# Second layer of a graph network: the split product, the rounding engine and the order of a chunk's steps

## The chip, the cores and the metric

One core of one Trainium2 chip. The metric is the device time of one execution in microseconds, as the median of the runs; lower is better. The engines are TensorE (PE; PEld is its weight load), VectorE (DVE), ScalarE (ACT), GpSimd (POOL) and SyncE (SP), which issues most DMAs. An engine's name with a q behind it is its instruction queue.

## The reference

Two graph layers with pre-norm over 12500 nodes of 128 values and 400000 edges that are sorted by destination. The first is an edge MLP with sums per destination. The second, cut to what matters here:

```python
h = jnp.maximum(_layernorm(x, axis=-1), 0.0)
H = jnp.einsum('ni,rio->rno', h, W)            # 8 relations, 128 x 128 each
msg = (H[etype, src] + b[etype]) * norm        # 400000 messages of 128
out = jax.ops.segment_sum(msg, dst, num_segments=h.shape[0])
x = x + jax.nn.relu(out)
```

`norm` is a weight per edge. All data are float32.

## The kernel before

**Work of the second layer.** The first layer's nodes go into a table in DRAM, `tab_h`, with RX = 9 blocks of 128 values in each row: eight blocks `H[r] + b[r]` for the eight relations and, as the ninth, the node's new x (`rows_h`, lines 546 to 567). Seen as rows of one block each (`tab_hr`), the message of an edge is row `src * 9 + etype`; these indices are prepared during the first layer (`hidx`, cast to integers in `hidx_sb` at line 646).

Edges are cut into tiles of P = 128, chunks of CT = 8 tiles (1024 edges) and spans of SC = 3 chunks; there are 3128 tiles, 391 chunks and 131 spans, the last of one chunk. A span's destinations lie within a window of 128 nodes. Within one partition of a chunk the eight edges stand in their order, so they have at most two destinations, the first edge's and the last's.

**One chunk** (`layer1_once`, lines 956 to 1040). GpSimd issues eight indirect DMAs, one a tile, which gather 128 rows of 512 bytes into `hg` (line 1019; five buffers). VectorE multiplies the 128x1024 tile by the edges' weights, twice: once with the weights of the edges that have the first destination (q = 0) and once with the rest (q = 1) (line 1026, into `v` in PSUM). After each product it sums the eight tiles (line 1030) into `sm`, also in PSUM. ScalarE copies `sm` to `hm` in SBUF and rounds it to fp32r, TensorE's fast float format (line 1033). VectorE subtracts to get the part lost in rounding (line 987) and builds two 128x128 one-hot matrices from the two destinations (line 989). TensorE multiplies one by the other into `acc` of the span (line 994).

These last steps are `sum_up`. The program puts them off by one chunk: a chunk's call goes into the list `todo` and runs behind the next chunk's first product.

**End of a span.** `write` reduces `acc` to the sums (line 505), takes relu and adds x, which an SP DMA has read from the table (`x1_of`, line 848), and stores the 128 rows of output (`to_out`, lines 853 and 854). Nodes that a span shares with the next are added by two small matmuls (`carry`, line 500) from the sums before.

**Order.** A scheduler orders the instructions of each engine unless the program pins them. `in_order(start, engines)` pins: it ties each instruction since `start` to the one before it on the same engine, without a wait on the chip. It looks at the list of the block that was current at the kernel's start. `layer1_once` stands in the body of an `If` on a flag (line 1044), whose instructions are collected in a block of their own, so that by the code the call at its end finds none of them.

The flag says whether the edges fit the windows above; otherwise the loops of `again` would run. They don't run here.

Of the kernel before, what the change touches and what calls it, by code (L numbers as in the profile page):

```python
# [14 lines left out]
OP = mybir.AluOpType  # L15
AX = mybir.AxisListType
ENG = mybir.EngineType
# [3 lines left out]
P = 128  # L21
D = 128
DE = 64
R = 8
# [5 lines left out]
NP = P * NJ  # L30
GJ = 7
CT = 8
CE = CT * P
SC = 3
ST = SC * CT
NT = -(-E // P)
NC = -(-E // CE)
# [12 lines left out]
ROW = 4 * D  # L50
# [3 lines left out]
def gnn_kernel(  # L54
# [34 lines left out]


    nc = tc.nc
    block = nc.cur_bb
    queues = {}

    def traced():
        return len(block.bb.instructions)

    def in_order(start, *engines):

        for i in block.bb.instructions[start:]:  # L100
            if i.engine in engines:
                if i.engine in queues:
                    tc.add_manual_dep(
                        i, queues[i.engine].name,
                        mybir.DependencyInfo(mybir.DependencyClass.NoSync,
                                             mybir.DependencyReason.DATA), reason="in order")
                queues[i.engine] = i

    start = traced()
# [8 lines left out]
    tab_h = dram.tile([NP + P, RX * D], F32, name="tab_h")  # L118
# [24 lines left out]
    b_f = const.tile([P, R * D], F32, name="b_f")  # L143
# [23 lines left out]
    def in_bytes(v):  # L167
        return v.bitcast(U8)
# [20 lines left out]
    with tc.tile_pool(name="n0", bufs=2) as pool, \  # L189
# [48 lines left out]
        for i, (xg, (g, n)) in enumerate(zip(xs, groups)):  # L238
# [4 lines left out]
            k = g - g0  # L243
# [302 lines left out]
    def rows_h(pool, psum, to, x0, aw, banks, out_row=None):  # L546

        ht = pool.tile([P, RX * D], F32, name="ht1", bufs=2)
        x1 = ht[:, R * D:]
        nc.vector.tensor_add(x1, x0, aw)  # L550
        if out_row is not None:
            nc.sync.dma_start(out[ds(out_row, P), :], x1)
        mv, sd = deviation(pool, x1)
        yield
        t = normed(pool, x1, mv, sd)
        yield
        pt = psum.tile([P, 512], F32, name=banks[0])
        nc.tensor.transpose(pt[:, 0:P], t, ident)
        hT = pool.tile([P, P], F32, name="hT1", bufs=2)
        nc.scalar.activation(hT, pt[:, 0:P], AF.Relu)  # L560
        for k in range(2):
            cols = slice(512 * k, 512 * k + 512)
            yield
            ph = psum.tile([P, 512], F32, name=banks[1 + k])
            nc.tensor.matmul(ph, hT, w_f[:, cols], start=True, stop=True)
            nc.vector.tensor_add(ht[:, cols], ph, b_f[:, cols])  # L566
        nc.sync.dma_start(to, in_bytes(ht))


    with tc.tile_pool(name="e0", bufs=2) as pool, \  # L570
# [39 lines left out]
        def prepare():  # L610

            nc.sync.dma_start(w_f.rearrange("i (r o) -> i r o", r=R), w.rearrange("r i o -> i r o"))
            yield
            nc.sync.dma_start(b_f, b.to_broadcast([P, R * D]))
            yield
            for g in range(0, NTP, QT):
                m = min(QT, NTP - g)
                cols = slice(g, g + m)
                for given, table in ((dst_t, dst_d), (et, hidx_d), (ew, ew_d)):
                    raw = pool.tile([P, QT], F32, name="raw", bufs=1)  # L620
                    nc.sync.dma_start(raw[:, :m] if given is ew else raw[:, :m].bitcast(I32),
                                      given[:, cols])
                    yield
                    if given is dst_t:
                        nc.vector.tensor_copy(raw[:, :m], raw[:, :m].bitcast(I32))
                    elif given is et:
                        nc.vector.scalar_tensor_tensor(raw[:, :m], src_sb[:, cols], float(RX),
                                                       raw[:, :m].bitcast(I32),
                                                       op0=OP.mult, op1=OP.add)
                    tr = pool.tile([P, QT], F32, name="tr", bufs=1)  # L630
                    nc.vector.transpose(tr[:, :m], raw[:, :m])
                    rows = table[cols, :].rearrange("(q r) (a j) -> a r q j", r=32, j=32)
                    for a in range(4):
                        nc.sync.dma_start(
                            rows[a], tr[32 * a:32 * a + 32, :m].rearrange("r (q j) -> r q j", j=32))
                    yield
            odd = pool.tile([P, NSP // QS], F32, name="odd", bufs=1)
            for i, s in enumerate(range(0, NSP, QS)):
                cols = slice(s * ST, (s + QS) * ST)
                hidx = pool.tile([P, QS * ST], F32, name="hidx", bufs=1)  # L640
                for table, to in ((dst_d, rel_t[:, cols]), (hidx_d, hidx), (ew_d, ew_sb[:, cols])):
                    nc.sync.dma_start(to.rearrange("p (c k) -> p c k", k=CT),
                                      table[cols, :].rearrange("(c t) (q k) -> (t q) c k",
                                                               t=CT, k=CT))
                    yield
                nc.vector.tensor_copy(hidx_sb[:, cols], hidx)
                rel = rel_t[:, cols]
                nc.vector.tensor_sub(rel.rearrange("p (s t) -> p s t", t=ST),
                                     rel.rearrange("p (s t) -> p s t", t=ST),
                                     base[:, s:s + QS, None].to_broadcast([P, QS, ST]))  # L650
                yield
                rel = rel.rearrange("p (c k) -> p c k", k=CT)
                off = []
                for k in (0, CT - 1):
                    o = pool.tile([P, QS * SC, CT], F32, name="off")
                    nc.vector.tensor_sub(o, rel,
                                         rel[:, :, k:k + 1].to_broadcast([P, QS * SC, CT]))
                    off.append(o)
                nc.vector.tensor_mul(off[0], off[0], off[1])
                nc.vector.tensor_mul(off[0], off[0], off[0])  # L660
                nc.vector.tensor_reduce(odd[:, i:i + 1], off[0].rearrange("p c k -> p (c k)"),
                                        AX.X, OP.max)
                yield
            most = pool.tile([P, 1], F32, name="most", bufs=1)
            nc.vector.tensor_reduce(most, odd, AX.X, OP.max)
            nc.sync.dma_start(odd_d.rearrange("o p -> p o"), most)
            yield
            odds = pool.tile([1, P], F32, name="odds", bufs=1)
            nc.sync.dma_start(odds, odd_d)
            yield  # L670
            nc.vector.tensor_reduce(vm[:, 1:2], odds, AX.X, OP.max)
            worst = pool.tile([1, 1], F32, name="worst", bufs=1)
            nc.vector.tensor_reduce(worst, vm, AX.X, OP.max)
            nc.vector.tensor_scalar(bad, worst, 0.0, None, op0=OP.is_gt)
            yield
            zeros = pool.tile([P, D], F32, name="zeros", bufs=1)
            nc.vector.memset(zeros, 0.0)
            nc.sync.dma_start(tab_h[NP:NP + P, R * D:], zeros)

        class Span:  # L680

# [163 lines left out]
    def x1_of(pool, rows):  # L845

        xw = pool.tile([P, D], F32, name="xw1", bufs=3)
        nc.sync.dma_start(in_bytes(xw), rows[:, R * ROW:])
        return xw

    def to_out(pool, sums, xw, to):
# [104 lines left out]
    def layer1_once():  # L956
# [4 lines left out]
        with tc.tile_pool(name="e1", bufs=2) as pool, \  # L961
# [2 lines left out]
            io_p = psum.tile([P, 512], F32, name="io_p", bufs=1)  # L964
            iota_p = io_p[:, 0:P]
            nc.vector.tensor_copy(iota_p, iota_f)
            todo = []
            open_s = []
            before = [None]

# [32 lines left out]
            for c in range(NC):  # L1003
# [19 lines left out]
                t = c % (WS * SC) * CT  # L1023
                for q in range(2):
                    v = psum.tile([P, CT, D], F32, name="v1", bufs=1)
                    nc.vector.tensor_tensor(  # L1026
                        v, hg, w_p[:, q, t:t + CT, None].to_broadcast([P, CT, D]), op=OP.mult)
                    if todo:
                        sum_up(*todo.pop())
                    nc.vector.tensor_reduce(sm[:, q, :], v.rearrange("p t d -> p d t"),  # L1030
                                            AX.X, OP.add)
                hm = pool.tile([P, 2, 2, D], F32R, name="hm2", bufs=6)
                nc.scalar.copy(hm[:, :, 0, :], sm)  # L1033
                ends = rel_t[:, c * CT:c * CT + CT:CT - 1][:, :, None]
                todo.append((s, acc, sm, hm, ends, k == 0, k == SC - 1 or c == NC - 1))
                if len(open_s) > 1 and (k == SC - 1 or c == NC - 1):
                    write()
            sum_up(*todo.pop())
            write()
            in_order(start, ENG.SP, ENG.DVE, ENG.Activation, ENG.PE)  # L1040

    flag = nc.values_load(bad[0:1, 0:1], min_val=0, max_val=1,
                          skip_runtime_bounds_check_because="it is 0 or 1")
# [66 lines left out]
```

## Time and profile before

| | us |
|---|---|
| median of 5 runs | 7953.2 (7951.66 to 7957.37) |
| the profiled execution | 7955.49 |
| its span in the trace | 7953.7 |
| first gather of the second layer starts | 4031.5 |
| last gather of the second layer starts | 7936.1 |
| mean length of a gather on GpSimd, second layer | 0.944 |
| VectorE busy between 5000 and 6000 us | 567.8 |
| GpSimd busy between 5000 and 6000 us | 755.9 |
| ScalarE busy between 5000 and 6000 us | 37.3 |

How to read it: the span is what the trace holds of one execution; the execution's own time is a little more. Busy time is the time in which an instruction ran on an engine; an engine that is busy three quarters of the time may still never wait for another, if it pauses between its own instructions. A group of instructions has its line in the code, engine, operation, what it writes and reads, and behind the bar its busy time, the mean of one in ns, and the idle time before it with what ended that. The chain that ended last is followed back from the last instruction, at each step to what released it.

### The profile page before, as it was taken

How to read it: one execution, taken by the hardware profiler on the slowest of the kernel's cores; microseconds unless marked ns; L12 is line 12 of the kernel's file. 1: busy time of each engine (PE TensorE's matmuls, PEld its weight loads, DVE VectorE, ACT ScalarE, POOL GpSimd, SP SyncE). 2: the span in 40 equal slices, each digit the busy share in tenths (PEclk: the TensorE clock that was granted, in tenths of full speed). 3: DMA queues.
4: the chain of work that ended last, by engine and by line, in shares of the span. 5: the costliest groups of instructions: out<-in, count | busy, mean ns of one | idle time of the engine just before them, and what ended most of it. 6: DMA issues, size and time to landing. Idle time of an engine off the chain costs nothing.

```text
span 7953.7 us, 56126 instructions
## 1 busy us (share of the span) xinstructions
PE 3688.1 (46%) x13981; PEld 1812.7 (23%) x13982; DVE 5276.7 (66%) x8291; ACT 1689.7 (21%) x3217; POOL 5953.6 (75%) x6273
## 2 busy tenths in 40 slices
PE   4888888888888888888820111111111101111111
PEld 2443443433444434333310000000000000000000
DVE  7887777777777777777755555555555555555555
ACT  3443333333333333333300000000000000000000
POOL 6777777777777777777757777777777777777776
PEclk7999898989999899899965555555555555555555
DMA  5555433333333333333322222222222222222222
GB/s 162 139 103 102 92 92 94 86 91 94 83 94 93 85 94 88 89 94 85 93 55 57 57 57 57 57 57 57 57 57 57 57 57 57 57 57 57 57 57 53
DMA packets 605554, 614.49 MB, mean 77 GB/s; under 512 B 361632, under 2 KB 465892, under 8 KB 604766
## 3 DMA queue, kind: packets, MB, share of 16 engines
q0 software_dynamic: 200192, 256.65, 15.1%
q1 hardware_dynamic: 403064, 353.77, 14.8%
q8 instruction: 114, 1.87, 0.1%
q14 instruction: 220, 1.80, 0.1%
q10 hardware_dynamic: 1964, 0.41, 0.0%
HBM read 509.91 MB, written 100.43 MB: 77 GB/s over the span
## 4 chain that ended last, share of the span: by engine, by line
POOL 49%; issue 23%; DVE 11%; DMA 10%; PE 5%; ACT 2%; DVEq 0%; POOLq 0%; ACTq 0%; SPq 0%
POOL hg L1019 32%; POOL gb L387 17%; DMA gb<-tab_a,src_sb 8%; DVE ohT L406 2%; DVE nm L480 2%; DVE oh L485 2%; DMA hg<-tab_h,hidx_sb 1%; DVE z L431 1%; PE pq L466 1%; PE acc L494 1%; ACT nm L475 1%; DVE pq L474 1%; DVE agT L427 1%; PE pm L442 1%; DVE ht L566 1%
## 5 line engine op out<-in xcount | busy, mean ns | idle before, releaser
L1019 POOL DMA_INDIRECT hg<-tab_h,hidx_sb x3128 | 2952.7, 944 | 996.7 <-issue 938.8
L387 POOL DMA_INDIRECT gb<-tab_a,src_sb x3032 | 2868.5, 946 | 925.6 <-issue 795.9
L1026 DVE TENSOR_TENSOR v<-hg,io_p 128x1024 f32<-128x1024 f32 x782 | 959.9, 1228 | 1621.1 <-DMA hg<-tab_h,hidx_sb 1612.2
L994 PE MATMUL acc<-hm,oh 128*128 128x256 f32 x782 | 347.5, 512 | 3516.0 <-DVE oh L989 3482.8
L994 PEld LDWEIGHTS acc<-hm,oh 128*128 128x128 f32 x782 | 205.7, 303 | 3676.8 <-issue 3641.7
L1030 DVE TENSOR_REDUCE sm<-v 128x128 f32<-128x1024 f32 x782 | 958.5, 1226 | 9.0
L1033 ACT CAST hm<-sm 128x256 fp32r<-128x256 f32 x391 | 145.7, 373 | 3777.3 <-DVE sm L1030 3777.3
L466 PE MATMUL pq<-w_n,h 128*128 128x256 f32 x3128 | 849.9, 421 | 0.0
L466 PEld LDWEIGHTS pq<-w_n,h 128*128 128x128 f32 x3128 | 649.6, 218 | 91.5 <-issue 0.9
L480 DVE SCALAR_TENSOR_TENSOR nm<-pq,nm 128x512 fp32r<-128x512 f32 x782 | 503.7, 686 | 243.8 <-ACT nm L475 214.0
L494 PE MATMUL acc<-nm,oh 128*128 128x256 f32 x3128 | 595.7, 329 | 110.8 <-DVE nm L480 66.4
L494 PEld LDWEIGHTS acc<-nm,oh 128*128 128x128 f32 x3128 | 466.3, 214 | 503.7 <-issue 207.0
L474 DVE TENSOR_TENSOR pq<-pq,b_n 128x512 f32<-128x512 f32 x782 | 509.5, 693 | 50.2 <-PE pq L466 50.0
L447 ACT ACTIVATE em<-pm,b_e 128x512 f32<-128x512 f32 x782 | 492.1, 681 | 207.4 <-PE pm L442 207.0
L459 ACT ACTIVATE h<-u,b_n 128x512 f32<-128x512 f32 x391 | 268.7, 687 | 1257.9 <-PE u L456 1257.9
L427 DVE STREAM_TRANSPOSE agT<-gb 128x256 f32<-128x256 f32 x391 | 173.5, 444 | 529.6 <-DMA gb<-tab_a,src_sb 516.0
L475 ACT ACTIVATE nm<-pq 128x512 fp32r<-128x512 f32 x782 | 432.4, 591 | 351.5 <-DVE pq L474 349.1
L420 PE MATMUL pre<-eats,w_ea 128*64 128x512 f32 x782 | 459.0, 671 | 98.6 <-DMA win<-tab_cb 93.2
L442 PE MATMUL pm<-h,w_e 32*128 32x512 f32 x1564 | 496.6, 714 | 1.0 <-ACT h L435 1.0
L406 DVE TENSOR_TENSOR ohT<-relb,io_p 126x1024 bf16<-126x1024 bf16 x391 | 477.6, 1222 | 18.4 <-DMA relb<-rel_d 6.4
L485 DVE TENSOR_TENSOR oh<-io_p,rel_s 128x1024 fp32r<-128x1024 f32 x391 | 476.0, 1217 | 0.0
L456 PE MATMUL u<-em,w_msg 128*64 128x512 f32 x1564 | 405.0, 596 | 3.3 <-ACT em L447 3.3
(122 smaller groups left out, 3474.8 us busy)
## 6 DMA issues: line engine op xcount, KB each, us to landing
eats<-in_ea SPq DMA_DIRECT2D x131, 768.0 KB
relb<-rel_d SPq DMA_DIRECT2D x131, 756.0 KB
tab_h<-ht SPq DMA_DIRECT2D x131, 576.0 KB
hg<-tab_h,hidx_sb POOLq DMA_INDIRECT x3128
gb<-tab_a,src_sb POOLq DMA_INDIRECT x3032
win<-tab_cb SPq DMA_DIRECT2D x391, 23.6 KB
xt<-in_x SPq DMA_DIRECT2D x131, 64.0 KB
xw<-tab_h SPq DMA_DIRECT2D x131, 64.0 KB
```

Of the source, the lines that this page charges most:

```text
L387: nc.gpsimd.indirect_dma_start(out=gb[:, t, :], out_offset=None, in_=tab_a, in_offset=bass.IndirectOffsetOnAxis(ap=idx(t), axis=0))
L406: nc.vector.tensor_tensor(self.ohT, relb, self.node.to_broadcast([WR, CE]), op=OP.is_equal)
L442: nc.tensor.matmul(pm, w_e2[rows, :], self.h1[rows, :], start=True, stop=True)
L466: nc.tensor.matmul(pq[:, 2 * i:2 * i + 2, :], self.h2[:, P * (2 * k + i):P * (2 * k + i) + P], w_n2, start=True, stop=True)
L474: nc.vector.tensor_add(pq, pq, b_n2[:, None, :].to_broadcast([P, 4, D]))
L480: nc.vector.scalar_tensor_tensor(nm[:, :, 1, :], pq, 0.0, nm[:, :, 0, :], op0=OP.max, op1=OP.subtract)
L485: nc.vector.tensor_tensor(self.oh, self.iota[:, None, :].to_broadcast([P, CT, P]), rel[:, :, None].to_broadcast([P, CT, P]), op=OP.is_equal)
L494: nc.tensor.matmul(acc, self.oh[:, i, :], self.nm[:, at, :, :].rearrange("p q d -> p (q d)"), start=(start and i == 0), stop=(stop and i = ...
L994: nc.tensor.matmul(acc[:, 0:2 * D], oh[:, q, :], hm[:, q, :, :].rearrange("p r d -> p (r d)"), start=begin and q == 0, stop=stop and q == 1)
L1019: nc.gpsimd.indirect_dma_start(out=hg[:, t - c * CT, :], out_offset=None, in_=tab_hr, in_offset=bass.IndirectOffsetOnAxis(ap=hidx_sb[:, t: ...
L1026: nc.vector.tensor_tensor(v, hg, w_p[:, q, t:t + CT, None].to_broadcast([P, CT, D]), op=OP.mult)
L1030: nc.vector.tensor_reduce(sm[:, q, :], v.rearrange("p t d -> p d t"), AX.X, OP.add)
```

## The change

- `in_order` takes the block that is current where the order begins, and in the second layer it pins SP, VectorE and TensorE (ScalarE has no instruction there any more).
- A chunk's first product (q = 0) is split: the last tile first, then the other seven. The second product stays whole.
- VectorE copies and rounds `sm` to `hm`, not ScalarE.
- `sum_up` runs at the end of its own chunk, not behind the next chunk's first product. `write` runs in the first chunk of the next span, ahead of that chunk's `sum_up`.
- In the table's rows, x is the first block, not the last; the indices of the messages are one more, which takes an addition where a cast was.

```diff
     nc = tc.nc
-    block = nc.cur_bb
     queues = {}
 
     def traced():
-        return len(block.bb.instructions)
+        block = nc.cur_bb
+        return block, len(block.bb.instructions)
 
     def in_order(start, *engines):
 
-        for i in block.bb.instructions[start:]:
+        block, at = start
+        for i in block.bb.instructions[at:]:
...
         ht = pool.tile([P, RX * D], F32, name="ht1", bufs=2)
-        x1 = ht[:, R * D:]
+        x1 = ht[:, 0:D]
...
-            nc.vector.tensor_add(ht[:, cols], ph, b_f[:, cols])
+            nc.vector.tensor_add(ht[:, D:][:, cols], ph, b_f[:, cols])
...
-                nc.vector.tensor_copy(hidx_sb[:, cols], hidx)
+                nc.vector.tensor_scalar(hidx_sb[:, cols], hidx, 1.0, None, op0=OP.add)
...
-            nc.sync.dma_start(tab_h[NP:NP + P, R * D:], zeros)
+            nc.sync.dma_start(tab_h[NP:NP + P, 0:D], zeros)
...
-        nc.sync.dma_start(in_bytes(xw), rows[:, R * ROW:])
+        nc.sync.dma_start(in_bytes(xw), rows[:, 0:ROW])
...
-            todo = []
             open_s = []
...
                     v = psum.tile([P, CT, D], F32, name="v1", bufs=1)
-                    nc.vector.tensor_tensor(
-                        v, hg, w_p[:, q, t:t + CT, None].to_broadcast([P, CT, D]), op=OP.mult)
-                    if todo:
-                        sum_up(*todo.pop())
+
+                    for at, n in ((CT - 1, 1), (0, CT - 1)) if q == 0 else ((0, CT),):
+                        nc.vector.tensor_tensor(
+                            v[:, at:at + n, :], hg[:, at:at + n, :],
+                            w_p[:, q, t + at:t + at + n, None].to_broadcast([P, n, D]), op=OP.mult)
                     nc.vector.tensor_reduce(sm[:, q, :], v.rearrange("p t d -> p d t"),
                                             AX.X, OP.add)
                 hm = pool.tile([P, 2, 2, D], F32R, name="hm2", bufs=6)
-                nc.scalar.copy(hm[:, :, 0, :], sm)
+                nc.vector.tensor_copy(hm[:, :, 0, :], sm)
                 ends = rel_t[:, c * CT:c * CT + CT:CT - 1][:, :, None]
-                todo.append((s, acc, sm, hm, ends, k == 0, k == SC - 1 or c == NC - 1))
-                if len(open_s) > 1 and (k == SC - 1 or c == NC - 1):
+                if k == 0 and s:
                     write()
-            sum_up(*todo.pop())
+                sum_up(s, acc, sm, hm, ends, k == 0, k == SC - 1 or c == NC - 1)
             write()
-            in_order(start, ENG.SP, ENG.DVE, ENG.Activation, ENG.PE)
+            queues.clear()
+            in_order(start, ENG.SP, ENG.DVE, ENG.PE)
```

## The prediction

> **What bounds the kernel now.** I read the page from its totals to the chain that ended last, then the second layer's groups, then the trace of one chunk and of the end. Totals and chain first:
>
> ```profile
> PE 3688.1 (46%) x13981; PEld 1812.7 (23%) x13982; DVE 5276.7 (66%) x8291; ACT 1689.7 (21%) x3217; POOL 5953.6 (75%) x6273
> ...
> POOL 49%; issue 23%; DVE 11%; DMA 10%; PE 5%; ACT 2%; DVEq 0%; POOLq 0%; ACTq 0%; SPq 0%
> ```
>
> The chain is GpSimd's busy time plus "issue", the pause between two of its instructions for which the profile shows no wait. The groups say which instructions these are (busy, mean ns of one, idle before and its releaser):
>
> ```profile
> L1019 POOL DMA_INDIRECT hg<-tab_h,hidx_sb x3128 | 2952.7, 944 | 996.7 <-issue 938.8
> ...
> L1026 DVE TENSOR_TENSOR v<-hg,io_p 128x1024 f32<-128x1024 f32 x782 | 959.9, 1228 | 1621.1 <-DMA hg<-tab_h,hidx_sb 1612.2
> ...
> L1030 DVE TENSOR_REDUCE sm<-v 128x128 f32<-128x1024 f32 x782 | 958.5, 1226 | 9.0
> L1033 ACT CAST hm<-sm 128x256 fp32r<-128x256 f32 x391 | 145.7, 373 | 3777.3 <-DVE sm L1030 3777.3
> ```
>
> GpSimd issues one gather after another and waits for nobody: of its 996.7 us of idle, 938.8 are issue pauses of 0.30 us. VectorE waits 1612.2 us for gathered rows, ScalarE 3777.3 us for VectorE. One chunk in the timeline (start us, length us; idle before and its releaser in brackets):
>
> ```profile
> 5011.73 0.94 POOL L1019 DMA_INDIRECT hg<-tab_h,hidx_sb  x1 [0.30 <-issue]
> 5011.92 1.23 DVE L1026 TENSOR_TENSOR v<-hg,io_p 128x1024 f32<-128x1024 f32 x1 [4.39 <-DMA hg<-tab_h,hidx_sb]
> 5012.98 0.94 POOL L1019 DMA_INDIRECT hg<-tab_h,hidx_sb  x1 [0.30 <-issue]
> 5013.06 0.41 DVE L987 TENSOR_TENSOR hm<-sm,hm 128x256 fp32r<-128x256 f32 x1
> 5013.40 0.41 DVE L989 TENSOR_TENSOR oh<-io_p,rel_t 128x256 fp32r<-128x256 f32 x1
> ...
> 5016.24 1.23 DVE L1030 TENSOR_REDUCE sm<-v 128x128 f32<-128x1024 f32 x1
> ...
> 5017.59 0.37 ACT L1033 CAST hm<-sm 128x256 fp32r<-128x256 f32 x1 [9.77 <-DVE sm L1030]
> ```
>
> VectorE sits 4.39 us idle before a chunk; GpSimd goes straight on. The first gather starts at 4031.54, the last at 7936.08 (the two ends of the line's group): 3904.54 / 3127 = 1.2487 us each, 9.99 us for a chunk's eight. The spacings of the starts have a median of 1.249, a 99th percentile of 1.254 and a maximum of 1.320 us. **So the second layer is 3128 gathers at 1.2487 us, and only what comes before the first or after the last is free to move otherwise.** What comes after is 7953.70 - 7936.08 = 17.62 us, with these pieces in its chain of waits:
>
> ```profile
> 7936.08 2.73 DMA hg<-tab_h,hidx_sb
> ...
> 7938.93 1.23 DVE v L1026
> 7940.16 0.33 DVE hm L987
> 7940.49 0.34 DVE oh L989
> ...
> 7945.59 0.38 ACT hm L1033
> ...
> 7948.57 0.29 DVE o L853
> ```
>
> The rows land at 7938.81; the last VectorE instruction ends at 7948.86, 10.05 us later. In between stand the previous chunk's subtract and one-hot, and ScalarE's copy.
>
> **The change part by part.**
>
> *Rounding on VectorE.* Removes 391 ScalarE casts of 0.373 us, adds 391 VectorE copies 128x256 from PSUM. None is in the trace; the nearest rows are VectorE copies 128x128 at 0.294 us and 128x384 from PSUM at 0.543. These are the bounds; in between, 0.294 + 0.249/2 = 0.42, which is also what the subtract of this very tile takes (0.418). I take 0.42.
>
> *Last tile first.* One 128x1024 product becomes one of 128x128 and one of 128x896. Bounds for the small one: 0.247 (128x96) to 0.367 (the 128x128 tensor_scalar of line 536, mean); I take 0.283, the 128x128 row of line 853. For the large one: 0.854 (128x672) to 1.228; I take 1.074, the 128x896 row of line 251. Together +0.13 us a chunk. The product now waits for eight landings through four queue waits of 0.05 us; the small one needs the last tile alone, the other seven are waited for behind it, while it runs. Queued behind it is the chunk's own work, which needs those tiles in any case.
>
> VectorE per chunk before: 2 x 1.228 + 2 x 1.226 + 0.418 + 0.414 = 5.74, plus a third of the span's 0.418 + 0.283 (0.23) and a twelfth of the weights' 0.767 (0.06): 6.04 us. After: 6.04 + 0.13 + 0.42 = 6.59, with the bounds above 6.2 to 6.9. The chunk's period is 9.99. **Cost in the steady state: nothing; the cover is VectorE's wait for rows.** It would be gone at 9.99 us a chunk, 3.4 us above my figure; from there each further 0.04 us a chunk is 16 us in all. Nor is GpSimd held by buffers: today a chunk's rows are last read 4.3 us after their landing (5011.92 to 5014.98 + 1.23), with the new order 0.28 + 1.07 + 1.23 + 1.23 = 3.8 us, and with five buffers a buffer is needed again only 40 us after it was filled.
>
> *Program order on SP, VectorE and TensorE.* It moves instructions. The subtract, one-hot and two matmuls of a chunk go from behind the next chunk's first product to the end of their own chunk, 5 to 6 us earlier; all lie in VectorE's idle time. The span's reduce, relu-add and output DMA stay in the next span's first chunk, now behind its copy. The wait of that reduce for TensorE (63.3 us over 100 spans, none on the chain) goes, since its matmuls are a chunk old; late next is again the gather. On SP the x load of a span stands ahead of the previous span's output; it needs a buffer that came free a span ago, and nothing on GpSimd reads from SP. Cost 0.
>
> *x as the first block.* Same 128x4608-byte row store, same 512-byte pieces read back; SP saves one address addition of 0.037 us a span, off the chain. Twelve casts 128x264 become tensor_scalar adds; casts cost 0.264 to 0.473 us, mean 0.302. Bounds -0.2 to +0.2 us each, 2.4 us in all, during the first layer, where GpSimd again sets the pace. I take 0.
>
> *The stretch between the layers.* The first gather starts 1.23 us after the last table store lands (4030.31); six queue waits of 0.04 us and VectorE's first weights lie in it. Three "is" products were drawn forward there; in program order one remains, so the first gather may gain, if it does wait for VectorE: bounds -0.8 to +0.3 us. I take 0, the row of the queue waits being nearer.
>
> *The end.* Spacing of dependent VectorE instructions is length + 0.03, of independent ones length - 0.08 (from the timeline). After landing: 0.12 to the start, 0.20 small product, 1.10 large, 3 x 1.265 for reduce, product, reduce, 0.34 copy, 0.45 span reduce, 0.20 relu-add, 0.34 subtract, 0.56 one-hot to the first matmul, 1.64 matmuls with the carry (7946.47 to 7948.11), 0.46 and 0.29 for the last reduce and add: 9.50 against 10.05, **-0.5 us**. What goes is the previous chunk's subtract and one-hot; what is late next is VectorE itself.
>
> **Sum**, on the profiled execution's 7955.49 us (span 7953.70 and 1.79 around it): 7955.49 + 0 - 0.5 = 7955.0. The median of the runs, 7953.2, lies 2.3 below that execution, so I forecast 7952.7 for a median.
>
> **A rule that speaks against this.** The row: the first layer runs two VectorE operations with one SBUF input and SBUF output beside gathers, the tensor_scalar of line 536 and the cast of line 646. Gathers that overlap line 536 (326 spacings) are 1.2497 us apart in the mean, 1.317 at most: up to 0.068 us is lost once, 0.001 in the mean. The Trainium skill, "SBUF — State Buffer", section "SBUF: two separate sides", warns that a VectorE copy in a two-port mode locks GpSimd out of the shared port and so starves the descriptors of a DMA that GpSimd issues. By that alone, 391 copies of 0.42 us would add up to 164 us, 8117. "VectorE: DVE Perf Modes", "Mode 2×_2P", limits that mode to operands in SBUF, and the copy here reads PSUM; by this it adds nothing. The trace leans to the second: beside the subtract of line 987, which writes the same tile from the same PSUM tile, the mean spacing is 1.2486 us (474 spacings), no more than elsewhere.
>
> **Rivals.**
> 1. *The copy delays GpSimd* (slower). Place: the gathers issued beside the new copy that takes the place of line 1033. Price by line 536's worst: 391 x 0.068 = 26.6 us, so 7979; by its mean 0.4 us. It decides from 0.041 us a copy (16 us). Against it: line 987. Chance 0.05.
> 2. *The stretch between the layers shrinks* (faster). From the last gather of layer one (3986.68) to the first of layer two there are 44.9 us; the end has 17.6. A gain of 16 us would have to come from the former, but the chain there is VectorE, TensorE and the store of the table's rows, which the change doesn't shorten. Worked out: 7953 - 16 = 7937 at the deciding point. Chance 0.02.
> 3. *The order doesn't bind or the scheduler's is as good*: then the end keeps its 10.05 us plus 0.13 for the split: 7953.3. Same side; chance 0.2 within the likeliest case.
>
> **How the numbers follow.** Within 0.2% (15.9 us, about what a measurement of this kernel can tell from no change): 0.93, of it 0.73 for the forecast and 0.2 for rival 3; slower 0.05; faster 0.02. Range: the runs before spread from 7951.7 to 7957.4; terms of -0.8 to +0.3 between the layers, 0 to -1 at the end and 2.4 for the casts give 7949 to 7958, which holds over 8 in 10 without the other cases.
>
> **What would show it.** Right: spacing of gathers 1.2487 us still; VectorE's wait for rows 0.5 us less per chunk (some 1400 us left in all); no ScalarE line in layer two; the end some 0.5 us shorter. Wrong: gathers that overlap the new copy spaced by more than 1.25; GpSimd waiting for VectorE; a first gather that starts anywhere but within 1 us of 4031.5.

## The result and the profile after

The changed kernel takes 7958.86 us (median of 24 runs, 7955.26 to 7966.15), the kernel before 7955.54 us (median of 44 runs, 7951.66 to 7957.82). The ratio is 1.0005 with a 95% interval of 0.9999 to 1.001: within 0.2%, as forecast, but 3.3 us up and not 0.5 down. The forecast of 7952.7 missed by 6.2 us, and the range of 7949 to 7958 by 0.9.

The profiled execution of the changed kernel took 7953.85 us with a span of 7952.0, 1.7 us shorter than that of before. This one pair therefore points the other way. The trace shows why: the pair differs in the first layer too, which the change hardly touches. From here on the second layer is measured by itself, from the start of its first gather to the start of its last.

| | before | after |
|---|---|---|
| first gather of the second layer starts | 4031.54 | 4026.63 |
| first gather to last gather | 3904.54 | 3908.37 |
| last gather's start to the end of the span | 17.65 | 17.01 |
| spacings of gathers over 1.27 us, of 3127 | 1 | 71 |

The second layer got 3.8 us longer and the end 0.6 us shorter: together 3.2, which is what the medians show.

Totals of the page and the groups of the second layer (busy, mean ns, idle before and its releaser):

```profile
PE 3691.1 (46%) x13981; PEld 1813.3 (23%) x13982; DVE 5596.3 (70%) x9073; ACT 1543.5 (19%) x2826; POOL 5952.9 (75%) x6273
...
POOL 48%; issue 23%; DVE 12%; DMA 9%; PE 7%; ACT 2%; DVEq 0%; POOLq 0%; ACTq 0%; SPq 0%
...
L1019 POOL DMA_INDIRECT hg<-tab_h,hidx_sb x3128 | 2956.4, 945 | 996.5 <-issue 942.9
```

ScalarE has lost its 146 us in the second layer, VectorE has gained 320. The row of the gathers hides the news almost wholly: its mean goes from 944 to 945 ns. The same groups on VectorE, with shapes kept apart, in the second layer:

```profile
L1028 DVE TENSOR_TENSOR v<-hg,io_p 128x1024 f32<-128x1024 f32 x391 | 480.3, 1228 | 13.5
L1028 DVE TENSOR_TENSOR v<-hg,io_p 128x896 f32<-128x896 f32 x391 | 428.6, 1096 | 36.6 <-DVE v L1028 6.9
L1034 DVE CAST hm<-sm 128x256 fp32r<-128x256 f32 x391 | 165.8, 424 | 13.5
...
L1028 DVE TENSOR_TENSOR v<-hg,io_p 128x128 f32<-128x128 f32 x391 | 115.8, 296 | 1271.1 <-DMA hg<-tab_h,hidx_sb 1271.1
L506 DVE TENSOR_REDUCE a<-acc 128x128 f32<-128x256 f32 x131 | 54.0, 413 | 1.8 <-PE acc L994 1.8
L854 DVE SCALAR_TENSOR_TENSOR o<-a,xw 128x128 f32<-128x128 f32 x131 | 39.2, 299 | 4.5
```

The copy takes 0.424 us and the two parts of the first product 0.296 and 1.096, so VectorE still has 1271 us in which it waits for rows. The line that matters is one that got no attention: the span's relu-add of line 854. Its mean rose from 283 to 299 ns and its longest from 321 to 368. One place where it runs, in a span's second chunk of gathers on GpSimd (start, length, in us):

```profile
4072.82 0.94 POOL L1019 DMA_INDIRECT hg<-tab_h,hidx_sb  x1 [0.30 <-issue]
4073.19 0.42 DVE L1034 CAST hm<-sm 128x256 fp32r<-128x256 f32 x1
4073.53 0.41 DVE L506 TENSOR_REDUCE a<-acc 128x128 f32<-128x256 f32 x1
4073.98 0.29 DVE L854 SCALAR_TENSOR_TENSOR o<-a,xw 128x128 f32<-128x128 f32 x1
4074.06 1.03 POOL L1019 DMA_INDIRECT hg<-tab_h,hidx_sb  x1 [0.30 <-issue]
...
4075.39 0.94 POOL L1019 DMA_INDIRECT hg<-tab_h,hidx_sb  x1 [0.30 <-issue]
```

The gather at 4074.06 takes 1.03 us, not 0.94, and the next starts 1.33 us after it. All 71 long spacings belong to the same gather of a span, the seventh in the second chunk, and in each one the relu-add of line 854 had begun 0.04 to 0.14 us before that gather started. The profile puts down no wait: the loss is inside the gather's own busy time, where neither the list of waits nor the idle column can show it. The 71 are 5.0 us late in all; the other spacings have a mean of 1.2483 us against 1.2486 before, which gives 1.2 us back. Whether that small gain belongs to the change is open: the ten profiles of the changed kernel and its versions at ordinary speed have 1.2482 to 1.2484 us, but of the kernel before there are only two such profiles, one at 1.2486 and one at 1.2504.

The end is as it was worked out. In the chain of waits of the changed kernel:

```profile
7935.00 2.74 DMA hg<-tab_h,hidx_sb
...
7943.06 0.07 DVE hm L1034
...
7947.03 0.29 DVE o L854
```

Rows land at 7937.74, the last VectorE instruction ends at 7947.32: 9.58 us, where 9.50 was forecast and 10.05 stood before.

### The profile page after: what moved, and what is told of

Same layout as the page of the kernel before. It is cut to its first block, busy times and chain, and to the rows that moved or that the text cites. A ratio compares the mean times of both kernels' runs of the same rounds, so it can differ in the third digit from the quotient of the medians.

```text
span 7952.0 us, 55770 instructions
## 1 busy us (share of the span) xinstructions
PE 3691.1 (46%) x13981; PEld 1813.3 (23%) x13982; DVE 5596.3 (70%) x9073; ACT 1543.5 (19%) x2826; POOL 5952.9 (75%) x6273
## 4 chain that ended last, share of the span: by engine, by line
POOL 48%; issue 23%; DVE 12%; DMA 9%; PE 7%; ACT 2%; DVEq 0%; POOLq 0%; ACTq 0%; SPq 0%
POOL hg L1019 33%; POOL gb L388 15%; DMA gb<-tab_a,src_sb 8%; DVE ohT L407 2%; DVE oh L486 2%; DVE nm L481 2%; PE pq L467 2%; DVE z L432 2%; PE acc L495 1%; DMA hg<-tab_h,hidx_sb 1%; DVE pq L475 1%; ACT nm L476 1%; PE pm L443 1%; DVE agT L428 1%; PE pre L421 1%
## 5 line engine op out<-in xcount | busy, mean ns | idle before, releaser
L1028 DVE TENSOR_TENSOR v<-hg,io_p 128x128 f32<-128x128 f32 (+2 forms) x1173 | 1024.7, 874 | 1321.2 <-DMA hg<-tab_h,hidx_sb 1271.1
L566 PE MATMUL u<-w_f,hT 128*128 128x512 f32 x520 | 293.4, 646 | 210.2 <-ACT h L460 209.0
```

The lines of the kernel that those rows point to most:

```text
L1028: nc.vector.tensor_tensor(v[:, at:at + n, :], hg[:, at:at + n, :], w_p[:, q, t + at:t + at + n, None].to_broadcast([P, n, D]), op=OP.mult)
```

## The experiments

**Theory A**: the span's relu-add reads two SBUF tiles (the sums and x). Early in a gather GpSimd has to read from SBUF as well (the indices in `hidx_sb`), and it can't while such an instruction of VectorE runs. In before the relu-add lay in the middle of a gather (0.29 us after its start in the median) and did no harm; the change brings it to 1.146 us after a start, so that it runs across the next start. **Rival B**: VectorE's new copy holds GpSimd up. **Rival C**: no difference, only scatter.

The table gives every run's count of spacings over 1.27 us, the length of the second layer from first to last gather, and the median's difference to the kernel before on the same chip. A difference of a few us lies inside the interval of its ratio (about 0.1% to each side, 8 us), so the counts and lengths from the trace decide, and the times only where they are larger. Two runs that took 9.8 ms stand further below and not in the table.

| run | long spacings | second layer, us | to before, us |
|---|---|---|---|
| the changed kernel again | 72 | 3908.67 | +4.0 |
| write behind | 2 | 3903.46 | -0.6 |
| sums in PSUM | 0 | 3903.48 | -0.5 |
| every chunk | 240 | 3919.71 | +15.7 |
| long, two in SBUF | 387 | 4119.11 | +219.3 |
| long, one in SBUF | 72 | 3907.73 | +6.2 |
| second copy | 0 | 3903.28 | -0.3 |
| round on ScalarE | 1 | 3903.52 | -2.0 |
| whole product | 0 | 3903.27 | -0.6 |
| before again | 1 | 3910.14 | +1.7 |

**The changed kernel again**, without an edit.

> The changed kernel once more. Theory A (the span's relu-add, which reads two SBUF tiles, now starts about 0.1 us ahead of a gather and holds that gather up): 60 to 80 of the second layer's 3127 gather spacings over 1.27 us, all at the seventh gather of a span's second chunk, together 4 to 6 us, mean spacing 1.2497 to 1.2501; time 2 to 5 us over before. Rival B (the VectorE copy holds GpSimd up): the same total, but delays in any chunk. Rival C (no real difference, chip scatter): the number of long spacings falls to a handful, as in the kernel before (1), and the time is within 1 us of before.

Measured: 72 long spacings, all at the seventh gather of the second chunk, 5.3 us late in all; mean spacing 1.24997 us; 7957.17 against 7953.21 us, ratio 1.0005 (0.9996 to 1.0014). The count repeats, so C falls for the trace; and with copies in every chunk but delays at one gather of a span only, B has little left.

**Write behind.** Only the place of the span's reduce and relu-add changes.

```diff
-                if k == 0 and s:
+                if c == NC - 1:
                     write()
                 sum_up(s, acc, sm, hm, ends, k == 0, k == SC - 1 or c == NC - 1)
+                if k == 0 and s and c < NC - 1:
+                    write()
```

> The span's reduce, relu-add and output come behind the chunk's subtract and one-hot instead of ahead of them, so the relu-add starts some 0.67 us later, in the middle of a gather. Theory A: at most 10 spacings over 1.27 us, mean spacing 1.2483 to 1.2487, time 3 to 5 us below the changed kernel and within 1.5 us of before. Rival B: 70 long spacings stay, since each chunk still has its copy at the same place. Rival C: no difference between this and the changed kernel.

Measured: the relu-add starts 0.71 us after a gather's start in the median; 2 long spacings are left, at the two spans where it came late enough to run across the next start. Second layer 3903.46 us, 4.9 less than the changed kernel. The copies are all there, so B falls.

**Sums in PSUM.** The relu-add keeps its place, its shape and its output; one input moves.

```diff
-                before[0] = summed(pool, acc, "a2")
-                to_out(pool, before[0], xw, to)
+                sums = acc[:, 2 * D:3 * D]
+                nc.vector.tensor_reduce(sums, acc[:, 0:2 * D].rearrange("p (q d) -> p d q", q=2),
+                                        AX.X, OP.add)
+                to_out(pool, sums, xw, to)
+                before[0] = pool.tile([P, D], F32, name="a2", bufs=2)
+                nc.vector.tensor_copy(before[0], sums)
```

> The relu-add stays at its place but reads the sums from PSUM, so it has one SBUF input instead of two; an added copy 128x128 of the sums to SBUF comes behind it. Theory A: at most 10 long spacings although the relu-add still starts 1.05 to 1.22 us after a gather's start; time 3 to 5 us below the changed kernel. If it is the start of any VectorE instruction at that place and not its two SBUF inputs: 70 long spacings stay. Rival B: 70 stay, or more with the added copy.

Measured: no long spacing. The relu-add still starts 1.136 us after a gather's start, and in 78 of 130 spans it begins at least 0.046 us before a gather and ends more than 0.128 us after that gather's start. In the changed kernel this was so in 80 spans, and 71 of these 80 gathers were late by more than 0.02 us. One of them, in the timeline (acc is the PSUM tile):

```profile
6441.22 0.29 DVE L854 SCALAR_TENSOR_TENSOR o<-acc,xw 128x128 f32<-128x128 f32 x1
6441.28 0.94 POOL L1023 DMA_INDIRECT hg<-tab_h,hidx_sb  x1 [0.30 <-issue]
...
6442.53 0.95 POOL L1023 DMA_INDIRECT hg<-tab_h,hidx_sb  x1 [0.30 <-issue]
```

The relu-add begins 0.06 us before the gather, as in the cases that lost 0.1 us, and the gather takes its 0.94. So place alone does nothing; for this instruction it needs the second SBUF input.

**Every chunk.** The dose is tripled; the extra results are not used.

```diff
                 if k == 0 and s:
                     write()
+                else:
+                    extra_a = pool.tile([P, D], F32, name="extra_a")
+                    nc.vector.tensor_reduce(extra_a, sm.rearrange("p q d -> p d q"), AX.X, OP.add)
+                    extra_o = pool.tile([P, D], F32, name="extra_o")
+                    nc.vector.scalar_tensor_tensor(extra_o, extra_a, 0.0, ew_sb[:, 0:D],
+                                                   op0=OP.max, op1=OP.add)
```

> The two chunks of a span that have no span reduce and relu-add get an extra pair of the same shapes at the same place (reduce 128x128 from 128x256 in PSUM, relu-add of two SBUF tiles 128x128), whose results are not used. Theory A: three times as many relu-adds at that place, so 3 x 71 = 200 (150 to 270) long spacings, 11 to 20 us in all, time 7 to 14 us above the changed kernel. Rival B: the number of copies is the same, so 71 long spacings and no change of the time. Rival C: no change.

Measured: 240 long spacings, 15.9 us late in all, spread over the three chunks of a span (81, 71 and 83 at the seventh gather, 5 elsewhere). Time 7968.93 against 7953.21 us, ratio 1.0019 (1.001 to 1.0028), 11.8 us above the changed kernel. Three times the dose, three times the loss.

**Long, two in SBUF, and its control.** A product 128x1024 behind the copy of each chunk, result not used:

```diff
                 nc.vector.tensor_copy(hm[:, :, 0, :], sm)
+                extra = pool.tile([P, CT, D], F32, name="extra")
+                nc.vector.tensor_tensor(extra, hg, hg, op=OP.mult)
```

The control takes its second input from PSUM, where v lies:

```diff
                 nc.vector.tensor_copy(hm[:, :, 0, :], sm)
+                extra = pool.tile([P, CT, D], F32, name="extra")
+                nc.vector.tensor_tensor(extra, hg, v, op=OP.mult)
```

> Behind each chunk's rounding copy VectorE also multiplies the gathered tile by itself, 128x1024, both inputs and the output in SBUF, result not used. It starts some 0.70 us after a gather's start, lasts 1.23 and so covers the start of the next gather. Theory A: that gather can't read its indices before the product ends, so one gather per chunk is 0.4 to 0.7 us late, 391 x 0.55 = 215 us (150 to 290), time 2 to 3.6% above before. If the extra work as such were to blame (VectorE 1.23 us busier a chunk, 7.8 of 9.99): no change, since VectorE has slack. Rival B (a copy or a write to SBUF blocks): about as much as in the run with one SBUF input.

> The control of the run with the long product of two SBUF tiles: same place, same shape, same output in SBUF, but one input is the product in PSUM. Theory A: no gather is late by it; time within 6 us of before (the relu-add's place moves with it, so 0 to 130 spacings over 1.27 us from that alone). If writing to SBUF or VectorE's load delays GpSimd: 150 to 290 us more, as in the run with two.

Measured, two in SBUF: 387 long spacings, 215.3 us late in all (215 were expected), time 8173.01 against 7953.7 us, ratio 1.0277 (1.026 to 1.0294). The control: 384 of its products begin 0.05 us or more before a gather and end 0.15 us or more after its start, and no gather is late by one; time 7959.88, ratio 1.0007 (0.9998 to 1.0017). The two side by side, first the one with both inputs in SBUF:

```profile
4090.92 1.21 DVE L1036 TENSOR_TENSOR extra<-hg 128x1024 f32<-128x1024 f32 x1
4091.41 1.54 POOL L1019 DMA_INDIRECT hg<-tab_h,hidx_sb  x1 [0.30 <-issue]
...
4093.25 0.94 POOL L1019 DMA_INDIRECT hg<-tab_h,hidx_sb  x1 [0.30 <-issue]
```

```profile
4090.63 1.21 DVE L1036 TENSOR_TENSOR extra<-hg,v 128x1024 f32<-128x1024 f32 x1
4091.09 0.94 POOL L1019 DMA_INDIRECT hg<-tab_h,hidx_sb  x1 [0.30 <-issue]
...
4092.33 0.94 POOL L1019 DMA_INDIRECT hg<-tab_h,hidx_sb  x1 [0.30 <-issue]
```

Same engine, shape, output and length; the gather that starts under it takes 1.54 us in the one and 0.94 in the other. VectorE's load (7.8 of 9.99 us a chunk in both) and its writes to SBUF are not the cause. The control has 72 long spacings from another source: the longer chunk moves the relu-add to 1.119 us after a gather's start, and it does there what it does in the changed kernel (4.4 us in all, now at the eighth gather). Of its +6.2 us the second layer shows 3.2 and the end 0.7; the rest is inside the scatter.

**Second copy.** Suspect B doubled:

```diff
                 nc.vector.tensor_copy(hm[:, :, 0, :], sm)
+                extra = pool.tile([P, 2, D], F32R, name="extra")
+                nc.vector.tensor_copy(extra, sm)
```

> A second copy of the sums from PSUM to SBUF behind each chunk's first one, result not used: 0.42 us more VectorE work per chunk. Theory A: the relu-add moves 0.34 us later, past the start of the gather, to some 0.24 us behind it: at most 10 long spacings, time 3 to 5 us below the changed kernel although work was added. Rival B: the copies are twice as many, so 140 long spacings and some 5 us above the changed kernel.

Measured: no long spacing, second layer 3903.28 us. The relu-add starts 0.24 us after a gather's start. Work was added to VectorE in every chunk and the layer got 5.1 us shorter than the changed kernel's. Ten of the 782 copies did lie across a gather's start, beginning 0.09 to 0.27 us before it and ending 0.16 to 0.32 us after it; these gathers took their 0.940 to 0.947 us. So B also falls where a copy stands at the critical place.

**Round on ScalarE.**

```diff
-                nc.vector.tensor_copy(hm[:, :, 0, :], sm)
+                nc.scalar.copy(hm[:, :, 0, :], sm)
```

> One part undone: ScalarE rounds again, the rest of the change stays. Theory A: the relu-add moves some 0.45 us earlier, to 0.7 us after a gather's start, and ends before the next gather begins: at most 10 long spacings, time 3 to 5 us below the changed kernel. Rival B: the VectorE copies are gone, so 0 to 10 long spacings too; this run doesn't tell A from B, it says whether the rounding on VectorE is the part that shifts the relu-add into its bad place.

Measured: relu-add at 0.70 us, 1 long spacing, second layer 3903.52 us.

**Whole product.** The split undone, run twice; the first time this kernel and the kernel before beside it took 9.8 ms:

```diff
-                    for at, n in ((CT - 1, 1), (0, CT - 1)) if q == 0 else ((0, CT),):
+                    for at, n in ((0, CT),):
```

> One part undone: the first product is whole again, the rest of the change stays. The chunk's steps then come some 0.24 us earlier against the gathers (one product of 1.26 us from start to start in place of 0.40 and 1.13), so the relu-add should start about 0.90 us after a gather's start, not 1.146, and end before the next gather reads. Theory A: at most 15 spacings over 1.27 us (the tail of the spread of the starts), second layer 3903 to 3905 us from first to last gather, time 2 to 5 us below the changed kernel. If the split itself costs nothing and the relu-add isn't the cause: 70 long spacings and the changed kernel's time.

> The kernel before, once more, for the scatter of its profile. At most 5 long spacings; 3903.3 to 3905 us from the second layer's first gather to its last; the first of them starts anywhere from 4026 to 4034 us.

Measured the first time: 9810.74 us, and the kernel before 9819.67 and 9811.29 in two sets of runs. Both kernels had over a thousand long spacings (1734 and 1200 in the profiles, at about 14 and 9 of a span's 24 gathers in nearly every span), and the first layer was 1.4 ms longer as well. What slowed them stays open; these runs tell nothing on the question.

> The run with the whole first product once more, since all kernels of that call, the one before among them, took 9.8 ms with gathers that were late for other reasons. Theory A: the relu-add starts about 0.90 us after a gather's start; at most 15 spacings over 1.27 us, 3903 to 3905 us from the second layer's first gather to its last, time 2 to 5 us below the changed kernel. If the split itself costs nothing and the relu-add isn't the cause: 70 long spacings and the changed kernel's time. If the call falls at 9.8 ms again, it stays open.

> The kernel before, once more, beside the run with the whole product. At most 5 long spacings; 3903.3 to 3905 us from the second layer's first gather to its last; the first of them starts anywhere from 4026 to 4034 us.

Measured the second time: whole product 7962.39 against 7962.94 us, relu-add at 0.95 us (0.90 expected), no long spacing, second layer 3903.27 us. The time was compared with the kernel before alone, so the expected gap to the changed kernel wasn't measured; the second layer's 5.1 us less stands for it. The kernel before: 1 long spacing, as expected, but a second layer of 3910.14 us, outside what was expected: all its gathers were 1.2504 us apart. Nearly all executions on that chip took about 7963 us, of both kernels; the profiled run of the whole product (7952.44) and one of the kernel before (7947.68) were the only ones far below. That is a drift of all gathers together and not the mechanism above.

None of the versions without the loss is measurably faster than the kernel before.

## Why the prediction was wrong

*GpSimd sets the pace, VectorE has slack.* Right. 3128 gathers still carry the layer, and VectorE waits 1271 us for rows. Some 1400 had been forecast: the lengths of its instructions rose by 238 us in the second layer, near the 215 of the sum, but of the lengths before 139 us had overlapped with one another, and of those after only 56. This costs no time.

*Rounding on VectorE, last tile first.* Sizes right: copy 0.424 us (0.42 forecast), small product 0.296 (0.283), large 1.096 (1.074). It was also right that they cost nothing as work. What they do is shift everything behind them in the chunk: undoing either one moves the relu-add back out of its bad place, and the loss is gone.

*"The span's reduce, relu-add and output DMA stay in the next span's first chunk, now behind its copy ... Cost 0."* **This is the step that failed.** The wait of the reduce for TensorE did go (63.3 us over 100 spans before, 1.8 now), and nothing waits for these instructions. But the step priced the move by who waits for whom, and not by what else the relu-add takes from GpSimd while it runs. It measured 5.0 us in 71 gathers, 3.8 net.

*Rival 1* had the right victim and the right way of losing time, but not the instruction: the copy held up no gather, and the relu-add did. The row that the rival took its price from, line 536, shows the same loss as the relu-add. Its worst case in the first layer of the kernel before:

```profile
2914.06 0.35 DVE L536 TENSOR_SCALAR t<-ht,mv,rs 128x128 f32<-128x128 f32 x1
2914.21 1.01 POOL L387 DMA_INDIRECT gb<-tab_a,src_sb  x1 [0.30 <-issue]
...
2915.53 0.95 POOL L387 DMA_INDIRECT gb<-tab_a,src_sb  x1 [0.30 <-issue]
```

It ends 0.197 us after the gather's start, and the gather takes 1.012 us and not 0.944: 0.068 late, which is the price the prediction read there. All ten of its cases that began 0.149 us or more before a gather and ended 0.135 us or more after its start delayed that gather, by 0.005 to 0.068 us; the cases that began later delayed none. The mean of 0.001 us over 326 spacings hid that the loss depends on place alone. In the same layer, behind the first 130 us, 68 gather spacings are over 1.27 us. The instructions that lie across the start of their gathers are most often those of lines 550 and 542, with 25 and 13 cases, and these are the two operations of the node step with two SBUF tensor inputs; line 536 follows with 7. So the trace of before held the right rows for the relu-add, but the prediction asked them only about the copy.

The rule was on the page that the prediction cites. The Trainium skill, "SBUF — State Buffer", section "Who interferes with whom", says that a VectorE instruction with two SBUF inputs contends with a GpSimd instruction that reads SBUF, since its second input comes through the shared read interface. The section "SBUF: two separate sides" says that whichever of the two starts first gets the shared ports for the whole instruction, and that the other fully blocks. The runs agree as far as VectorE comes first: the relu-add and the long product with two SBUF inputs delay the gather until they end, and neither does with one input in PSUM. Where the gather comes first they agree in part: relu-adds that begin between 0.044 us before a gather's start and 0.018 us after it are themselves longer, up to 0.368 us for 0.291, but one that begins 0.030 us after the start or later takes its usual 0.29 us beside the gather's 0.94. So a gather doesn't hold VectorE up for the whole of its length in the trace. That the lock is this interface is the page's statement; what the runs show is the dependence on the second SBUF input.

*Split as an early wait; buffers; SP's queue; x as the first block.* Nothing against any of them was seen: the whole product gains only through the relu-add's place, and GpSimd never waits for VectorE in the second layer. The casts as additions lie in the first layer, whose scatter of some 7 us hides 2.4; not tested by itself.

*The stretch between the layers.* 44.6 us from last to first gather against 44.9 before; 0 was forecast.

*The end.* -0.5 forecast, -0.6 measured.

*The range.* It rested on a median of five runs, 7953.2. The kernel before has a median of 7955.54 in 44 runs, so the profiled execution at 7955.49 was an ordinary one, and taking 2.3 us off it was wrong. Either error alone would have left the time inside the range; the two together, 2.3 and 3.8 with the end right, put it 0.9 us out. The sign "a first gather that starts anywhere but within 1 us of 4031.5" could tell nothing either: in ten profiles at ordinary speed besides those of before and after it starts between 4026.2 and 4033.7 us.

## What to carry to other kernels

When an instruction moves, ask not only who waits for it and on whom it waits, but also what it shares with the engine on the critical path while it runs, and against which phase of that engine's work it will now lie. Where a steady engine sets the pace, look at the spacing of its starts and not at its idle column: a loss inside its own instructions shows as a few long spacings, and the lines that run across the starts of the late ones name the cause. A mean over all spacings beside a line hides it. Before a long VectorE instruction with two SBUF tensor inputs is put beside a stream of GpSimd gathers, see whether one input can stay in PSUM. One SBUF input is no full safeguard, as line 536 shows. That the kernel before lost nothing here was luck of place: its relu-add also reads two SBUF tiles and happened to start 0.29 us into a gather.

## What the runs showed of the hardware

- A VectorE instruction with two SBUF tensor inputs that lay across the start of an indirect DMA on GpSimd delayed it. In 71 long gathers of the changed kernel, and in 387 of the run with the long product, the end of the VectorE instruction, counted from the gather's start, less the delay is 0.128 us in the median (0.118 to 0.133 over both). So the delay is the instruction's end minus 0.128 us, if it came first.
- In the changed kernel a relu-add came first if it began 0.047 us or more before the gather's start. The 20 that began from 0.044 us before to 0.018 us after the start left the gather at its 0.94 us and lasted 0.306 to 0.368 us themselves, until 0.321 to 0.324 us after that start.
- The same delay came from the tensor_scalar of line 536, which has one SBUF tensor input, two columns of scalars and its output in SBUF (ten cases in the trace of before). In the same trace 81 transposes from SBUF to SBUF (line 427) and 283 operations on a PSUM and an SBUF tile (line 474) that began 0.05 us or more before a gather and ended 0.15 us or more after its start delayed none.
- A steady stream on one engine and a chunk that is triggered by it keep a fixed phase: all 71 losses of the changed kernel came at the same gather of a span, and moving the relu-add by 0.20 us (whole product) to 0.45 us (rounding on ScalarE) switched them off.
- The pace of all gathers can shift by 0.17%, which is more than this change is worth: on one chip a profile of the whole product has a mean spacing of 1.2483 us and one of the kernel before 1.2504, and the times of both kernels there lie near 7950 us in single executions and near 7963 in the rest.
